# Seven half products for eight, moved from a kernel's second layer to the X and H parts of its first

## The chip, the cores and the metric

The kernel runs on one core of one Trainium2 chip, in one launch, in float32. The metric is the device time of the program in microseconds. The host only lays the inputs out.

## What is computed

The input x has 16 x 512 = 8192 rows of 512 values. Each row has a pathway token (500 kinds), a compartment token c (5) that also serves as its time step, and a mask bit that serves as its scale type m. The reference normalises the row, builds six blocks of 512 from it, weighs them by a softmax, puts them side by side (3072 values) and sends them through a network of two layers:

```python
h = _ln(x, pw_g[pathway_ids], pw_b[pathway_ids])
h = _ln(h, cp_g[compartment_ids], cp_b[compartment_ids])
t = _ln(x, tm_g[time_steps], tm_b[time_steps])
m = x + _mlp_ln(memory_state, ...)[:, None, :]       # n, r likewise from two other states
s = _ln(x, ms_g[scale_type], ms_b[scale_type])
cat = jnp.concatenate([w[0] * h, w[1] * t, w[2] * m, w[3] * n, w[4] * r, w[5] * s], axis=-1)
return x + _ln(silu(cat @ int_W1 + int_b1) @ int_W2 + int_b2, int_g, int_be)
```

## The kernel before, in words

**What is multiplied.** The six blocks come down to three parts of K = 512 each. Part X is x itself times one weight `wx_` (the blocks m, n and r share x). Part H is the twice normalised row times `wh_`. Part V is the once normalised row times a weight that depends on the row's two tokens (c, m): rows are sorted by these, so that a tile of 128 rows has (but for a few "extra" rows handled apart) one such weight, which is built for it as `vs = ws * s + wt * t` (`s_part` on ScalarE, `build` on VectorE). What is left of each block, with biases and the three states, is one row per kind, gathered from a table in DRAM (`gather_add`, the tile `add`).

**Tiles and windows.** The 8192 rows are 16 windows of four tiles of 128 rows. In each window four tiles are gathered (x by `gather_x`, the gains and shifts of the first norm by `gather_h`, which also gathers `cp`, those of the second), normalised, turned by VectorE's 32 x 32 transposes into `rX`, `rV`, `rH` (`turn`, L184), and spread by sixteen transfers for each part to `cX`, `cV`, `cH` (`spread_row`, L192, on SP's queue), so that K lies on the partitions. Layer 1 (`layer1`, L320) gives a tile 4 chunks x 3 parts of matmuls 128 x 128 times 128 x 512 into one PSUM tile. Then `hidden_add` (VectorE) adds the gathered row, `hidden_silu` (ScalarE) takes the activation, `turn_z` and `spread_row` make `cZ`, and layer 2 multiplies it by `w2`. `last_sum`, `last_var`, `last_pow` and `last_b` form the last norm, and `put_out` (GpSimd) scatters the rows to their places.

**Layer 2 before.** In windows 1 to 13 two tiles go together as a pair. Two tiles (rows), the two halves of K and the two halves of N make a 2 x 2 block product, done with seven half products for eight (Winograd's form): GpSimd forms sums of the operand in `z_sums` (L383 to L389, four of 128 x 256 for a pair), `weight_sums` formed those of `w2` once, `seventh` (L404, L406) multiplies with 256 columns, with the bias put in by a bfloat16 product of its own, and `keep_first`, `sum_first`, `keep_last` and `sum_last` (ScalarE copies, VectorE adds) put the four quarters together. In windows 0, 14 and 15 layer 2 is plain (`layer2`, L339).

**What sets the order.** Everything is issued in an order written out by hand as names: `ORDER` for the head, `WINDOW` once for each window (w = 0 to 14), `LAST` for the last. A name is a piece, a window (c the current, p the one before, n the next, o and m two before and after) and a tile or a pair and a number. Each engine and each DMA queue works its own pieces in this order; across engines they wait on semaphores. All normal transfers stand on SP's queue, all gathers and scatters on GpSimd's (POOL), among its arithmetic: `shift_x` (`sh`, L309), the powers (`fp`, `xp`, `lp`) and the sums.

Names that the prediction uses: `rd`, `la` reads of PSUM; `f1`, `f2` the two steps of the second norm on VectorE; `th`, `tv`, `tx`, `tz` transposes; `bd` build; `lb` end of the last norm; `gc`, `gh`, `ga`, `gx` gathers; `sh` shift_x; `sX`, `sZ` transfers; `p7`, `vp` products.

## Time and profile before

| | us |
|---|---|
| three runs | 976.53, 983.87, 984.45 |
| median | 983.87 |
| the profiled execution | 971.0 |
| its span, first to last instruction | 969.1 |
| TensorE busy in the span | 942.4 |
| VectorE busy | 820.2 |
| GpSimd busy | 653.1 |
| ScalarE busy | 571.5 |

The profile is of one execution. Busy time is the union of an engine's instruction records. A group's row gives line, engine, operation, out<-in, count, then busy time and mean ns of one, then the idle time of the engine ahead of it and what ended that. Records of instructions that follow each other overlap, as ends are pipelined; the pace is therefore read from the starts in the timeline. The mean granted clock of TensorE is 0.992.

### The profile page before, as it was taken

Reading aid. Unit: us, or ns where it says so; the run is one execution under the profiler, and the core shown is the slowest. Engines: PE = TensorE matmul, PEld = TensorE weight load, DVE = VectorE, ACT = ScalarE, POOL = GpSimd, SP = SyncE. Lnnn points to the kernel's source line nnn. Section 1 sums busy time; section 2 is a strip of 40 time slices with the busy share of each in tenths; the row PEclk is TensorE's granted clock in tenths of the full one; section 3 lists DMA queues with packets and bytes.
Section 4 is the critical chain, followed back from the end, with each engine's and each line's share of the span. In section 5 each row is a group of like instructions: output and inputs, shape, how many; then the busy total and the mean of one; then the engine's idle time right before and its main releaser. Section 6 shows DMA issues by size and latency. Waiting matters only on the chain.

```text
span 969.1 us, 11569 instructions
## 1 busy us (share of the span) xinstructions
PE 942.4 (97%) x2901; PEld 497.7 (51%) x2901; DVE 820.2 (85%) x1412; ACT 571.5 (59%) x1190; POOL 653.1 (67%) x697
## 2 busy tenths in 40 slices
...
GB/s 283 241 234 245 268 220 243 154 223 181 208 190 192 162 229 178 207 204 185 231 185 183 183 198 180 228 180 195 215 184 216 186 189 182 203 186 200 128 85 97
DMA packets 91885, 190.95 MB, mean 197 GB/s; under 512 B 25364, under 2 KB 25364, under 8 KB 91820
## 3 DMA queue, kind: packets, MB, share of 16 engines
...
## 4 chain that ended last, share of the span: by engine, by line
PE 84%; DVE 6%; DMA 5%; issue 2%; POOL 1%; SPq 1%; ACT 0%; POOLq 0%; ACTq 0%; DVEq 0%
PE p L320 62%; PE pq_0b L406 5%; PE pq_1b L406 5%; PE p L339 4%; PE pq_1a L406 3%; PE pq_0a L406 3%; DMA cH<-rH 2%; SPq L192 1%; DMA pw<-in_pw,i_pw 1%; DMA cX<-rX 1%; DVE vs L724 1%; POOL xbs L158 1%; DVE pw L283 0%; DMA pre<-diff_rows,tok_x 0%; DVE vs L226 0%
## 5 line engine op out<-in xcount | busy, mean ns | idle before, releaser
L320 PE MATMUL p<-wx__82,cX 128*128 128x512 f32 x512 | 227.9, 593 | 2.9 <-DVE adde L1118 2.9
L320 PE MATMUL p<-wh__83,cH 128*128 128x512 f32 x512 | 225.8, 593 | 1.8 <-DMA cH<-rH 1.7
L320 PE MATMUL p<-vs,cV 128*128 128x512 f32 x504 | 226.1, 592 | 0.0
L226 DVE SCALAR_TENSOR_TENSOR vs<-wt,sct,vs 128x512 f32<-128x512 f32 x252 | 175.8, 758 | 0.4 <-ACT vs L220 0.4
L220 ACT ACTIVATE vs<-ws,scs 128x512 f32<-128x512 f32 x252 | 164.1, 710 | 9.1 <-PE p L320 4.2
L320 PEld LDWEIGHTS p<-wx__82,cX 128*128 128x128 f32 x512 | 97.0, 190 | 125.3 <-issue 117.3
L320 PEld LDWEIGHTS p<-wh__83,cH 128*128 128x128 f32 x512 | 96.9, 190 | 114.6 <-issue 111.1
L320 PEld LDWEIGHTS p<-vs,cV 128*128 128x128 f32 x504 | 95.8, 190 | 115.0 <-issue 98.1
L327 ACT ACTIVATE add<-add 128x512 f32<-128x512 f32 x64 | 39.9, 625 | 158.2 <-DVE add L324 157.8
L497 POOL DMA_INDIRECT out<-yb,tok x64 | 71.5, 1116 | 76.4 <-DMA out<-yb,tok 27.9
L292 POOL TENSOR_TENSOR rsh<-veh,mhalf 128x1 f32<-128x1 f32 x64 | 42.3, 664 | 86.2 <-DVE vey L479 82.9
L158 POOL DMA_INDIRECT pw<-in_pw,i_pw x64 | 71.3, 1113 | 26.3 <-issue 12.5
L158 POOL DMA_INDIRECT xbs<-in_x,tok x64 | 68.4, 1069 | 24.3 <-issue 16.0
L309 POOL TENSOR_TENSOR xbs<-xbs,rows 128x512 f32<-128x512 f32 x64 | 81.7, 1279 | 0.8
L158 POOL DMA_INDIRECT add<-rows,i_add x64 | 69.0, 1078 | 16.6 <-issue 14.8
L158 POOL DMA_INDIRECT cp<-cp_rows,i_cp x64 | 63.3, 989 | 21.6 <-issue 17.7
L471 ACT ACTIVATE junk<-yb 128x512 f32<-128x512 f32 x64 | 39.9, 624 | 58.1 <-DVE yb L435 38.2
L324 DVE TENSOR_TENSOR add<-p,add 128x512 f32<-128x512 f32 x64 | 43.0, 673 | 24.7 <-PE p L320 24.6
L260 ACT ACTIVATE xm<-xbs,nmx,rsx 128x512 f32<-128x512 f32 x64 | 52.1, 815 | 19.7 <-DVE nmx L256 10.0
L296 ACT ACTIVATE pw<-pw,rsh 128x512 f32<-128x512 f32 x64 | 45.5, 713 | 26.4 <-POOL rsh L292 15.9
L301 DVE SCALAR_TENSOR_TENSOR pw<-pw,mvh,cp 128x512 f32<-128x512 f32 x64 | 60.4, 944 | 0.0
L238 ACT ACTIVATE junk<-xbs 128x512 f32<-128x512 f32 x72 | 44.7, 621 | 20.0 <-DMA xbs<-in_x,tok 19.0
...
## 6 DMA issues: line engine op xcount, KB each, us to landing
cV<-rV SPq DMA_DIRECT2D x256, 64.0 KB
cH<-rH SPq DMA_DIRECT2D x256, 64.0 KB
cZ<-rZ SPq DMA_DIRECT2D x256, 64.0 KB
...
```

What stands on the lines that cost most here:

```text
L158: nc.gpsimd.indirect_dma_start(dst, None, table, bass.IndirectOffsetOnAxis(ap=idx, axis=0), **kw)
L220: nc.scalar.activation(v[:, c], ws[:, c], AF.Identity, scale=scs[:, c, g, w : w + 1])
L226: nc.vector.scalar_tensor_tensor(v[:, c], wt[:, c], sct[:, c, g, w : w + 1], v[:, c], ALU.mult, ALU.add)
L238: nc.scalar.activation(junk, x, AF.Identity, accum_out=sums[:, 0, j : j + 1])
L260: nc.scalar.activation(t, st["xb"][:, j, :], AF.Identity, bias=st["nm"][:, j : j + 1], scale=st["rs"][:, j : j + 1])
L296: nc.scalar.mul(pw[:, :D], pw[:, :D], st.pop(("rs", j)))
L301: nc.vector.scalar_tensor_tensor(pw[:, :D], pw[:, :D], mv[:, 0, 0:1], cp, ALU.subtract, ALU.mult)
L309: nc.gpsimd.tensor_add(st["xb"][:, j, :], st["xb"][:, j, :], rows[:, 2, :])
L320: nc.tensor.matmul(st["p1", g], st["c" + blk][:, g, c, :], m[:, c, :], start=(blk == "X" and c == 0), stop=(blk == "H" and c == NC - 1))
L324: nc.vector.tensor_add(st["add", g], st["p1", g], st["add", g])
L406: nc.tensor.matmul(home, st["zp", p][k][:, c], at_["half"][k][:, c], start=False, stop=(c == 1), skip_group_check=True)
L497: nc.gpsimd.indirect_dma_start(out_rows, bass.IndirectOffsetOnAxis(ap=tok[:, j, w : w + 1], axis=0), yb[:, j, :], None)
```

## The change

- Layer 2 is plain again in all windows (`layer2`, then `last_add`); `z_sums`, `seventh`, the bias products and the four functions that put quarters together are gone.
- In windows 2 to 14 parts X and H of layer 1 together (K = 1024, of which X is the one half and H the other) become the 2 x 2 block product of a pair of tiles with seven half products (`xh_product`, 256 columns, four chunks each). The operand's sums are formed by GpSimd, in `cX` and `cH` themselves and in `s3` (four of 128 x 512 for a pair); those of `wx_` and `wh_` once in the head, in place, and undone ahead of the last window (`weights_back`).
- Part V is multiplied in two halves of N (`v_product`), one half into the banks of the pair's products, the other into a bank of its own.
- `hidden_add` is replaced in these windows by eleven adds of half width for a pair (`xh_read`), some of them between two products that add up in the same place.
- The mean and variance of the row ahead of the second norm come from two ScalarE passes (`front_sums`) for VectorE's batch statistics.
- The gather of `cp` is a step of its own (`gather_cp`), `cp` has two buffers for three; `xm` and `xn` share three buffers in place of two each; the two PSUM pools of four tiles become one of eight; `junk` is bfloat16; `ident` lives in the head only.
- `ORDER`, `WINDOW` and `LAST` are new.

```diff
 WINDOW = """
-    lX.c.3 lX.c.0 ha.p.3 hs.p.3 ga.c.2 lV.c.0 tz.p.2 xn.c.3 lb.o.3 gx.n.3 bd.c.1 xs.n.0 xn.c.2 po.o.2 sh.c.3 tz.p.3
-    xs.n.1 lX.c.1 lV.c.1 gx.n.2 gh.n.1 lX.c.2 f1.c.2 sp.c.2 sp.c.3 xs.n.3 f2.c.2 sZ.p.0 f1.c.3 f2.c.3 sZ.p.3 bd.c.2
-    lV.c.2 fp.c.3 fn.c.3 th.c.3 fp.c.2 po.o.3 ga.c.1 sZ.p.2 bd.c.3 xs.n.2 sZ.p.1 xe.n xp.n q7.p.1.1 zs.p.4 fn.c.2
-    th.c.2 sH.c.1 zs.p.0 zs.p.1 sp.n.0 sH.c.0 xm.n nv.n.1 tv.n.1 tx.n.2 q7.p.0.1 tx.n.1 zs.p.5 xn.n.1 q7.p.0.2
-    lV.c.3 kf.p.0 nv.n.3 kf.p.2 q7.p.0.5 tx.n.0 tx.n.3 kf.p.1 q7.p.1.5 zs.p.6 sH.c.3 sh.c.0 zs.p.7 f1.n.1 q7.p.1.6
-    nv.n.0 tv.n.3 sX.n.3 q7.p.0.7 ku.p.1 zs.p.2 q7.p.1.2 sf.p.2 kf.p.3 bd.n.0 q7.p.1.7 nv.n.2 tv.n.2 sH.c.2 f2.n.1
-    q7.p.0.6 q7.p.1.3 sX.n.1 sf.p.3 lH.c.1 ga.c.0 sh.c.1 tv.n.0 ha.c.1 lH.c.0 sl.p.2 ku.p.0 sf.p.1 sl.p.0 ha.c.0
-    zs.p.3 gh.n.0 q7.p.1.4 q7.p.0.4 gh.n.2 hs.c.1 xn.n.0 sl.p.3 lq.p.2 sf.p.0 lq.p.3 q7.p.0.3 sl.p.1 hs.c.0 sX.n.0
-    fp.n.1 lq.p.0 sh.c.2 fn.n.1 f1.n.0 lq.p.1 ga.c.3 lv.p tz.c.1 fp.n.0 lH.c.2 sp.n.1 th.n.1 ha.c.2 f2.n.0 lp.p
-    lb.p.1 sV.n.3 gh.n.3 hs.c.2 sV.n.1 po.p.1 lb.p.0 gx.m.0 sV.n.2 gx.m.1 sV.n.0 fn.n.0 lH.c.3 tz.c.0 lb.p.2 sX.n.2
-    po.p.0 th.n.0
+    gc.c.3 f1.c.3 p7.c.0.1 vp.c.0.0 xs.n.3 f1.c.2 sZ.p.1 gc.c.2 hb.c.3 xs.n.2 xe.n xp.n hb.c.2 po.o.3 xm.n vp.c.0.1
+    rd.c.0.0 sZ.p.0 p7.c.1.1 hv.c.3 vp.c.1.1 sZ.p.2 l2.p.1 ss.c.0.0 hv.c.2 sp.c.2 fp.c.3 la.p.1 nv.n.3 fp.c.2 xn.n.1
+    f2.c.2 sh.c.0 tv.n.3 nv.n.1 f2.c.3 sZ.p.3 tv.n.1 gc.n.1 gh.n.0 l2.p.0 la.p.0 ss.c.1.0 fn.c.3 th.c.3 l2.p.2
+    l2.p.3 fn.c.2 th.c.2 sH.c.3 f1.n.1 la.p.3 la.p.2 p7.c.0.7 nv.n.2 tv.n.2 rd.c.0.1 p7.c.1.7 sH.c.1 hb.n.1 hv.n.1
+    lq.p.3 vp.c.1.0 sh.c.2 lq.p.1 bd.c.2 rd.c.1.0 vp.c.2.1 lq.p.2 lq.p.0 rd.c.1.1 ss.c.1.1 sp.c.3 lv.p lp.p bd.c.3
+    tx.n.1 nv.n.0 gc.n.0 sH.c.2 p7.c.1.5 vp.c.3.0 ss.c.1.2 sH.c.0 xn.n.2 tv.n.0 f2.n.1 xn.n.0 lb.p.3 lb.p.0 tx.n.0
+    vp.c.3.1 sp.n.1 sV.n.3 rd.c.1.2 f1.n.0 rd.c.0.10 rd.c.0.9 hb.n.0 vp.c.2.0 fp.n.1 p7.c.0.2 lb.p.2 gh.n.3 ss.c.0.1
+    tx.n.2 sV.n.1 po.p.0 fn.n.1 gx.m.0 sV.n.0 sp.n.0 sV.n.2 lb.p.1 p7.c.1.2 tx.n.3 sX.n.0 ss.c.0.2 hv.n.0 ss.c.0.3
+    gx.m.1 ss.c.1.3 p7.c.0.5 rd.c.0.2 bd.n.0 gx.m.3 xn.n.3 rd.c.1.9 p7.c.1.6 rd.c.1.6 sX.n.2 p7.c.0.6 fp.n.0
+    rd.c.0.4 rd.c.1.3 p7.c.0.3 sh.c.1 sX.n.1 gx.m.2 xs.m.0 xs.m.1 gh.n.2 rd.c.0.5 rd.c.1.10 p7.c.1.3 po.p.1 rd.c.0.3
+    rd.c.1.7 ga.n.1 rd.c.1.5 th.n.1 rd.c.0.6 p7.c.0.4 rd.c.0.8 ga.n.2 hs.c.2 tz.c.2 sX.n.3 po.p.2 hs.c.1 p7.c.1.4
+    rd.c.0.7 rd.c.1.8 gh.m.1 ga.n.0 rd.c.1.4 ga.n.3 hs.c.3 f2.n.0 hs.c.0 tz.c.1 tz.c.3 tz.c.0 sh.n.3 fn.n.0 th.n.0
+    bd.n.1
 """
...
-    xnp = ctx.enter_context(tc.tile_pool(name="xnp", bufs=2))
+    xnp = ctx.enter_context(tc.tile_pool(name="xnp", bufs=3))
-    ps_1 = ctx.enter_context(tc.tile_pool(name="ps_1", bufs=4, space=bass.MemoryType.PSUM))
-    ps_2 = ctx.enter_context(tc.tile_pool(name="ps_2", bufs=4, space=bass.MemoryType.PSUM))
+    ps = ctx.enter_context(tc.tile_pool(name="ps", bufs=8, space=bass.MemoryType.PSUM))
...
+    def gather_cp(st, j):
+        w = st["w"]
+        st["cp", j] = cp = gp.tile([P, D], F32, tag="cp", name=f"cp{w}_{j}", bufs=2)
         gather(cp, cp_rows[:, :], i_cp[:, j, w : w + 1])
...
-        stats(mv, 0, pw[:, :D], P, "h")
+    def front_sums(st, j):
+        h = st["g", j][:, :D]
+        st["mv", j] = mv = small.tile([P, 3], F32, tag="mvh", name="mvh")
+        nc.scalar.activation(junk, h, AF.Identity, accum_out=mv[:, 0:1])
+        nc.scalar.mul(mv[:, 1:2], mv[:, 0:1], -1.0 / D)
+        nc.scalar.activation(junk, h, AF.Square, bias=mv[:, 1:2], accum_out=mv[:, 2:3])
...
+    def weight_sums(c):
+        H = D // 2
+        if "half" not in at_:
+            t = at_["late"].tile([P, 3, NC, H], F32, name="wxt")
+            at_["half"] = {1: wx_[:, :, :H], 2: wh_[:, :, :H], 3: wh_[:, :, H:], 4: t[:, 0], 5: wx_[:, :, H:],
+                           6: t[:, 1], 7: t[:, 2]}
+        b11, b21, b22, t4, t1, t2, t3 = [at_["half"][k][:, c] for k in range(1, 8)]
+        nc.gpsimd.tensor_sub(t3, b22, t1)
+        nc.gpsimd.tensor_sub(t1, t1, b11)
+        nc.gpsimd.tensor_sub(t2, b22, t1)
+        nc.gpsimd.tensor_sub(t4, b21, t2)
...
+    def xh_sums(eng, st, p, op):
+        t = xh_operands(st, p)
+        if op == 0:
+            eng.tensor_sub(t[-1], t[0], t[len(t) // 2])
+            return
+        a11, a12, a21, a22, _ = t
+        if op == 1:
+            eng.tensor_add(a21, a21, a22)
+        elif op == 2:
+            eng.tensor_sub(a11, a21, a11)
+        else:
+            eng.tensor_sub(a12, a12, a11)
...
+    def xh_product(st, p, k):
+        q1, q2 = xh_banks(st, p)
+        home = {1: q1[:, 0], 6: q1[:, 0], 2: q1[:, 1], 7: q2[:, 1], 4: q2[:, 1], 5: q2[:, 0], 3: q2[:, 0]}[k]
+        if k in (1, 5, 6):
+            m = st["cX"][:, 2 * p + (k == 5)]
+        elif k == 7:
+            m = st["s3"][:, p]
+        else:
+            m = st["cH"][:, 2 * p + (k == 4)]
+        for c in range(NC):
+            nc.tensor.matmul(home, m[:, c], at_["half"][k][:, c], start=(c == 0 and k in (1, 7)),
+                             stop=(c == NC - 1), skip_group_check=True)
+
+    def v_product(st, g, n):
+        p, b = divmod(g, 2)
         H = D // 2
+        q1, q2 = xh_banks(st, p)
+        home = v_bank(st, p)[:, b] if n else (q1, q2)[b][:, 1]
+        for c in range(NC):
+            nc.tensor.matmul(home, st["cV"][:, g, c], st["v", g][:, c, n * H : (n + 1) * H],
+                             start=(b == 0 and n == 1 and c == 0), stop=(c == NC - 1), skip_group_check=True)
+
+    def xh_read(st, p, i):
+        H = D // 2
+        q1, q2 = xh_banks(st, p)
+        a, b = st["add", 2 * p], st["add", 2 * p + 1]
+        half, bank = {0: (a[:, :H], q1[:, 0]), 1: (b[:, H:], q2[:, 1]), 2: (b[:, H:], q2[:, 0]),
+                      3: (a[:, H:], q1[:, 0]), 4: (b[:, :H], q1[:, 0]), 5: (b[:, H:], q1[:, 0]),
+                      6: (a[:, :H], q1[:, 1]), 7: (a[:, H:], q2[:, 0]), 8: (b[:, :H], q2[:, 1]),
+                      9: (a[:, H:], st.get(("pv", p), q1)[:, 0]), 10: (b[:, H:], st.get(("pv", p), q1)[:, 1])}[i]
+        nc.vector.tensor_add(half, bank, half)
```

Lines of the kernel after that the prediction names: L288 and L289 the two products of `front_1`, L312 `front_less`, L377 to L385 `xh_sums`, L427 `xh_read`.

280 lines of the change are left out of this document (110 added, 170 removed).

## The prediction

> **What bounds the kernel now.** I read the page's first part, then the busy time by stretches, then who waited for whom on TensorE, then TensorE's timeline.
>
> ```profile
> span 969.1 us, 11569 instructions
> PE 942.4 (97%) x2901; PEld 497.7 (51%) x2901; DVE 820.2 (85%) x1412; ACT 571.5 (59%) x1190; POOL 653.1 (67%) x697
> ```
> ```profile
> 0.00:100.00 100.00, 87.52 (x513) 53.52 (x514) 80.57 (x176) 79.26 (x194) 74.34 (x117) 0.95 0.82 252
> 100.00:200.00 100.00, 95.26 (x220) 41.13 (x220) 82.57 (x143) 52.58 (x97) 68.09 (x67) 1.00 0.77 218
> ```
> ```profile
> 207.00:877.00 670.00, 670.00 (x1956) 362.59 (x1955) 591.15 (x987) 402.19 (x825) 473.10 (x479) 1.00 0.69 195
> ```
> ```profile
> PE pc L660 <- DVE sm L666: 6.9, 1, 6.9
> ```
>
> In the rows of stretches the columns are start and end, length, then busy time of TensorE's matmuls, its weight loads, VectorE, ScalarE and GpSimd, the granted clock and the DMA share. From 207 to 877 us TensorE is busy for 670.00 of 670.00 us at a clock of 1.00. It is idle only in the head (12.5 us of the first 100, 4.7 of the second; the longest wait, 6.9 us, is its first) and behind the last product. So a window's time is TensorE's instruction count times their pace. VectorE comes next: 591.15/670 = 88%, which is 47.4 us of a window of 53.74. Pace and window come from the timeline:
>
> ```profile
> 575.15 3.60 PE L320 MATMUL p<-vs,cV 128*128 128x512 f32 x8
> 578.59 3.60 PE L320 MATMUL p<-wx__82,cX 128*128 128x512 f32 x8
> ...
> 592.32 0.28 PE L404 MATMUL pq_1a<-b2r,share 96*128 96x256 bf16 x1
> 592.43 1.03 PE L406 MATMUL pq_1a<-w,cZ 128*128 128x256 f32 x4
> ...
> 600.53 1.03 PE L406 MATMUL pq_1a<-w2t,zs 128*128 128x256 f32 x4
> 601.39 1.03 PE L406 MATMUL pq_0b<-w2t,zs 128*128 128x256 f32 x4
> ```
> ```profile
> 861.04 0.28 PE L404 MATMUL pq_1a<-b2r,share 96*128 96x256 bf16 x1
> ```
>
> An f32 matmul stands as two instructions. Eight with 512 columns step by 578.59 - 575.15 = 3.44 us, or 0.4294 each. Four with 256 columns step by 601.39 - 600.53 = 0.86, about 0.2155 each. Half the columns cost half, so products in half widths are nearly free of extra cost as long as the stream is unbroken. A bias product costs 592.43 - 592.32 = 0.11. The same product comes again five windows later, at 861.04: a window is (861.04 - 592.32)/5 = 53.74 us. The counts confirm the paces: 96 x 0.4294 + 56 x 0.2155 + 4 x 0.11 = 53.73.
>
> **TensorE's part of the change.** In a changed window (2 to 14, thirteen; layer 2 had its seven products in 1 to 13, thirteen too) layer 1 is 2 pairs x (7 products x 4 chunks + 16 for V) x 2 = 176 instructions of 256 columns: 37.93 us for 41.22. Layer 2 is 32 of 512 columns: 13.74 for 12.07 + 0.44. Sum 51.67 against 53.73: 2.06 a window, 26.8 in all. This is the gain if nothing makes TensorE wait.
>
> **What the others get.**
>
> ```profile
> L226 DVE SCALAR_TENSOR_TENSOR vs<-wt,sct,vs 128x512 f32<-128x512 f32 x252 | 175.8, 758 | 0.4 <-ACT vs L220 0.4
> L301 DVE SCALAR_TENSOR_TENSOR pw<-pw,mvh,cp 128x512 f32<-128x512 f32 x64 | 60.4, 944 | 0.0
> L283 DVE TENSOR_TENSOR pw<-xn,pw 128x512 f32<-128x512 f32 x64 | 51.3, 801 | 5.3 <-ACT xn L260 2.7 <-DMA pw<-in_pw,i_pw 2.5
> L284 DVE TENSOR_TENSOR pw<-pw 128x512 f32<-128x512 f32 x64 | 49.6, 775 | 2.2
> L163 DVE BATCH_NORM_STATS2 sth<-pw 128x6 f32<-128x512 f32 x64 | 44.5, 695 | 2.2
> L164 DVE BATCH_NORM_AGGREGATE mvh<-sth 128x2 f32<-128x6 f32 x64 | 11.7, 182 | 2.2
> L324 DVE TENSOR_TENSOR add<-p,add 128x512 f32<-128x512 f32 x64 | 43.0, 673 | 24.7 <-PE p L320 24.6
> L433 DVE TENSOR_TENSOR yb<-yb 128x256 f32<-128x256 f32 x26 | 21.8, 838 | 1.4
> L435 DVE TENSOR_TENSOR yb<-yb,pq_0b 128x512 f32<-128x512 f32 x13 | 8.9, 688 | 9.2 <-PE pq_0b L406 9.2
> L309 POOL TENSOR_TENSOR xbs<-xbs,rows 128x512 f32<-128x512 f32 x64 | 81.7, 1279 | 0.8
> L383 POOL TENSOR_TENSOR zs<-cZ 128x256 f32<-128x256 f32 x26 | 18.3, 718 | 0.3
> L389 POOL TENSOR_TENSOR zs<-cZ,zs 128x256 f32<-128x256 f32 x26 | 25.7, 990 | 0.0
> L238 ACT ACTIVATE junk<-xbs 128x512 f32<-128x512 f32 x72 | 44.7, 621 | 20.0 <-DMA xbs<-in_x,tok 19.0
> ```
> ```profile
> 607.46 0.70 DVE L301 SCALAR_TENSOR_TENSOR pw<-pw,mvh,cp 128x512 f32<-128x512 f32 x1
> 608.09 0.41 DVE L424 TENSOR_TENSOR yb<-yb,pq_1b 128x256 f32<-128x256 f32 x1
> 608.42 0.70 DVE L184 STREAM_TRANSPOSE rV<-xm 128x512 f32<-128x512 f32 x1
> 609.34 0.69 DVE L324 TENSOR_TENSOR add<-p,add 128x512 f32<-128x512 f32 x1 [0.22 <-PE p L320]
> 609.95 0.41 DVE L433 TENSOR_TENSOR yb<-yb 128x256 f32<-128x256 f32 x1
> 610.28 0.42 DVE L424 TENSOR_TENSOR yb<-yb,pq_0b 128x256 f32<-128x256 f32 x1
> 610.80 1.60 DVE L433 TENSOR_TENSOR yb<-yb 128x256 f32<-128x256 f32 x1
> ```
> ```profile
> 608.05 0.95 POOL L158 DMA_INDIRECT pw<-in_pw,i_pw  x1 [0.30 <-issue]
> 609.31 0.96 POOL L158 DMA_INDIRECT cp<-cp_rows,i_cp  x1 [0.30 <-issue]
> 610.84 1.27 POOL L309 TENSOR_TENSOR xbs<-xbs,rows 128x512 f32<-128x512 f32 x1
> ```
>
> VectorE's starts lie closer than its durations: a half-width add leads the next by 0.33 us (608.09 to 608.42), a full add or a transpose by 0.61 (609.34 to 609.95), a scalar-tensor-tensor by 0.63 (607.46 to 608.09). In a window it loses 4 statistics with their aggregates (0.695 + 0.182), 4 hidden adds (0.61), 4 half adds that end layer 2 (0.33), 2 sums of L433 (0.838) and 2 of L435 (0.61): 3.5 + 2.4 + 1.3 + 1.7 + 1.2 = 10.1. It gets 22 half-width reads of PSUM (`rd`) and 4 full adds (`la`): 7.3 + 2.4 = 9.7. That makes 47.0 of 51.67, where it had 47.4 of 53.74: its free time goes from 6.3 to 4.7.
>
> ScalarE gets the statistics, two passes of 0.62 or a little more for each tile (L238 is such a pass), and loses six half copies: it has 402.19/670 = 60% now, 32 us of a window, and stays under 40, covered. GpSimd's eight sums grow from 256 columns to 512: about 0.85 each (between L383 and L389) become 1.28 (L309), 3.4 more on 37.9 (473.10/670 of 53.74), so 41 of 51.67. The transfers are as many as before on the same queues. The gather of `cp` becomes a step of its own: POOL's queue is put in another order, not lengthened. SP's queue takes no new transfer, but its last sixteen of a window (`sX`) now wait for the last product that reads `cX`, `p7.c.0.6`, which ends 44.8 us into the window by the paces above.
>
> ```profile
> 602.00 2.42 SPq L192 DMA_DIRECT2D cX<-rX  x4
> ```
>
> Sixteen take 9.7, until 2.9 us into the next window; the four `sZ` behind them until 5.3, and layer 2 needs them at 8.6: covered, with 3.3 left for their landing. The weights' sums are sixteen of 256 columns in the head (11.5 us at 0.72) for four of 512 and the bias parts, on a GpSimd that is 68% busy there (second row of the stretches), and `wr` at the end stands beside layer 2: no cost.
>
> The buffers (three for `xn` and `xm` together, two for `cp`, one pool of eight in PSUM) cost nothing by themselves, only through the circles below.
>
> **The price: VectorE held up by GpSimd.** In the row at 610.80 an add that took 0.41 us at 609.95 takes 1.60, and ends just after GpSimd's sum (610.84 + 1.27 = 612.11). Adds that read PSUM do not show it: L324's mean, 0.673, is no longer than its single row at 609.34. What this costs now:
>
> ```profile
> L301 DVE SCALAR_TENSOR_TENSOR pw<-pw,mvh,cp x64: 702/741/2452, 64.7 to 906.8; 128x512 f32<-128x512 f32 x64
> ```
> In a window L301 loses 4 x (0.944 - 0.741) = 0.8 us so. L433 loses 2 x (0.838 - 0.41) = 0.85; L283 and L284, of the shape of L435 with its 0.688, lose 4 x (0.113 + 0.087) = 0.8; L226 at most 16 x (0.70 - 0.68) = 0.3. That is 2.7 a window, while GpSimd's sums run 4 x 1.28 + 8 x 0.85 = 11.9 us. With the change they run 12 x 1.28 = 15.4. In proportion that gives 3.5, a little less because L433 is gone: I take 3.2. The bounds are 1.8 (L433's part goes, nothing grows) and 7.7 (each of twelve catches an operation for half its length, 0.64). I stay near the lower one, as the operations that can be caught are those of these rows. The 47.0 above holds 1.8 already, so VectorE needs 48.4.
>
> The Trainium skill (SBUF — State Buffer, Who interferes with whom) has it as a lock: "A DVE instruction with two SBUF inputs contends with a GpSimd instruction that reads SBUF", and the loser waits out the whole instruction; the trace agrees (1.60 against 0.41 us). By that rule the 22 new PSUM reads are safe and the eight longer sums are not, which speaks against the change: taken to its end it is rival (c).
>
> **Two circles.** Each engine works its queue in order, so what counts is the longest circle through a window. (1) Layer 2's last product -> `la.p.3` on VectorE -> all of its queue to the last chunk of `bd.n.1` -> `vp` of tile 1 in the next window -> four layer-2 products. On VectorE: 2 la (1.2), 21 rd (6.9), 12 transposes (7.3), 2 f2 (1.3), one f1 (1.4), 4 lb (5.5), 16 chunks of build at 0.68 (10.9; 175.8/252 = 0.70 with L226's own hold-ups), small ones 0.5: 35.0. Then 0.43 for the last chunk, 13.74 for layer 2, 0.4 for hand-overs (the 0.22 of row 609.34, twice): 49.6, plus its share of the hold-ups, 2.6: 52.2. (2) `th.n.0` on VectorE frees a `pw` buffer -> POOL's queue: `gh`, two `ga`, `sh`, `gc`, `gc` -> landing -> `f2.c.2` -> VectorE to `th.n.0`.
>
> ```profile
> cp<-cp_rows,i_cp POOLq DMA_INDIRECT x64, 5.5
> add<-rows,i_add POOLq DMA_INDIRECT x64, 4.3
> ```
>
> Gathers leave 1.26 apart (608.05 to 609.31): 4 x 1.25 + 1.28 + a landing between 4.3 and 5.5 (`cp` stands behind the twice larger `pw` today, as `add` does not; I take 4.9) = 11.2; VectorE from `f2.c.2` to `la.p.3` 5.7 (2 f2, 4 transposes, a la, an f1), then the 35.0 without `bd.n.1`'s 2.7, together 38.0; hand-overs 0.3: 49.5, plus 3.0 of hold-ups: 52.5. Both pass TensorE's 51.67, so TensorE will wait about 0.8 a window. 53.74 - 52.5 = 1.24, x 13 = 16 us.
>
> **Sum.** Head and tail keep their matmuls; their orders are new, and TensorE's 17 us of head idle can move either way: taken as zero, 6 us each way in the range. The profiled execution took 971.0 us (span 969.1 and 1.9 around it); the runs' median, 983.87, is 1.3% above. The gain is taken off the median: 968. With hold-ups of 2.3 to 3.7 in the second circle this case spans 959 to 977.
>
> **Rivals.** (a) TensorE never waits: the planned order has enough room, as it had before (88% on VectorE, no wait in 670 us). For it: VectorE still has 51.67 - 48.4 = 3.3 us free. Against: the circles have only about 2 us of room for hold-ups. 983.9 - 26.8 = 957. (b) The circle through the gather is the long one with the 5.5 landing and hold-ups of 3.5: 53.6, gain 2 us: 982. For it: DMA is 0.69 busy. (c) Slower: GpSimd's sums catch VectorE two times in three at half length, 12 x 2/3 x 0.64 = 5.1: 54.6 a window, 0.9 x 13 = 11 us: 995. It decides from hold-ups of 4.2 a window on. For it: L301 already loses 2.452 - 0.741 = 1.7 us in its worst case. Against: now there are twelve such sums too, and they cost 2.7. (d) A doubled pace of 256 columns by weight loads is excluded: 0.2155 is measured.
>
> **Chances.** Forecast 0.36, (a) 0.26, (b) 0.19, (c) 0.19. The range from 953 to 990 leaves out the end of (a) and most of (c). A measurement of this kernel tells about 1% from no change: below 974 lie (a) and three quarters of the forecast, 0.53; within 1% 0.28; above 994 0.19, with the head's losses.
>
> **What would show it.** Steps of TensorE's timeline of 0.2155 and 0.4294 unchanged; window starts 52.5 apart; new TensorE waits on `vs` (build) and `cZ` of about 0.8 a window; L288, L312 (products ahead of H) longer than their medians beside POOL's sums at L377 to L385, PSUM reads at L427 not. Wrong would be: no waits at all (then 957), waits on POOL's sums themselves, or a head longer by over 6 us.

## The result and the profile after

| | before | after |
|---|---|---|
| median of 4 runs, us | 980.2 (976.08 to 984.45) | 1132.06 (1131.24 to 1134.16) |
| ratio, 95% interval | | 1.155 (1.148 to 1.162) |
| profiled span | 969.1 | 1129.5 |
| window (2 to 14) | 53.74 | 63.47 |
| span outside thirteen windows | 270.5 | 304.3 |

The change costs 152 us; 968 was predicted. The predicted window was 52.5 us. A window of the kernel after is read from one start of layer 2 in TensorE's timeline (222.76 us) to that thirteen windows later (1047.92). The page's first part, then the busy time of that stretch and of what lies outside it (columns as in the prediction):

```profile
span 1129.5 us, 13393 instructions
PE 986.7 (87%) x3577; PEld 652.2 (58%) x3577; DVE 920.4 (81%) x1466; ACT 656.2 (58%) x1432; POOL 712.8 (63%) x702
```
```profile
222.76:1047.92 825.16, 727.30 (x2682) 522.83 (x2681) 718.10 (x1106) 482.54 (x1036) 541.41 (x489) 0.96 0.59 164
```
```profile
0.00:222.76 222.76, 193.06 (x753) 101.03 (x754) 165.03 (x306) 153.89 (x355) 147.13 (x190) 0.94 0.74 221
1047.92:1129.50 81.58, 66.35 (x144) 28.32 (x144) 37.31 (x54) 19.75 (x44) 24.22 (x24) 0.90 0.26 78
```

825.16/13 = 63.47 us, 10.97 over the predicted 52.5. TensorE, never idle before, is idle for 825.16 - 727.30 = 97.9 us, and its matmuls take 727.30 for 13 x 51.67 = 671.7 at full pace, 55.6 us more. By the granted clock (0.96 on average) about 0.04 x 825 = 33 us of these are time lost at a lower clock, an estimate; the rest is not taken apart here. VectorE is busy for 718.10/13 = 55.2 us a window, where it was 47.4. The miss is (63.47 - 52.5) x 13 = 143 in the windows, 304.3 - 270.5 = 34 outside them, less the 13 by which the prediction's base, the median, stood above the profiled execution.

Who waits for whom, TensorE first, then VectorE in the thirteen windows (us in total, times, longest):

```profile
PE pq_0b L416 <- DVE add L427: 22.7, 13, 1.9
PE pq_1b L407 <- DVE add L427: 20.4, 12, 2.8
PE pq_0b L407 <- DVE add L427: 16.1, 8, 2.3
PE pq_1b L407 <- POOL s L377: 14.8, 12, 3.4
```
```profile
DVE nmx L261 <- POOL rsx L253: 43.8, 12, 6.1
DVE pw L312 <- DMA cp<-cp_rows,i_cp: 21.5, 13, 2.3
DVE vea L249 <- ACT junk L245: 19.4, 8, 2.4
DVE add L427 <- PE pq_1b L407: 1.4, 3, 0.7
```

TensorE waits mostly for VectorE's reads of PSUM (59.2 us in these rows), and 14.8 us for the first of GpSimd's sums (L377); VectorE waits for TensorE 1.4 us in 825. So TensorE no longer sets the pace. VectorE does, with 55 us of work a window and 63.47 - 55.2 = 8.2 us of standing still, in which it waits for GpSimd's power, the gather of `cp` and ScalarE's row sums. TensorE's waits, and with them its lower clock, follow from this. The groups of VectorE's work:

```profile
L231 DVE SCALAR_TENSOR_TENSOR vs<-wt,sct,vs 128x512 f32<-128x512 f32 x252 | 225.1, 952 | 0.0
L289 DVE TENSOR_TENSOR pw<-pw 128x512 f32<-128x512 f32 x64 | 77.6, 1213 | 2.2
L427 DVE TENSOR_TENSOR add<-pq_1a,add 128x256 f32<-128x256 f32 x65 | 26.7, 411 | 0.4
```

Build's mean went from 758 to 952 ns; the second step of the first norm, L289, from 775 (L284 before) to 1213. The reads of PSUM (L427) stay at 0.41. The trace's records, counted one by one, show that this is no general slowing: of the 208 builds in the thirteen windows, the 45 that overlap one of GpSimd's sums take 1.83 us on average, the other 163 take 0.74. The time by which such an instruction is longer is called a hold-up below. One such place, VectorE's rows first, then GpSimd's:

```profile
554.89 3.09 DVE L289 TENSOR_TENSOR pw<-pw 128x512 f32<-128x512 f32 x1
```
```profile
554.93 1.27 POOL L377 TENSOR_TENSOR s<-cX 128x512 f32<-128x512 f32 x1
556.15 1.27 POOL L320 TENSOR_TENSOR xbs<-xbs,rows 128x512 f32<-128x512 f32 x1
```

An add that takes 0.69 undisturbed (row at 601.86 below) takes 3.09 here and ends (557.98) after the second of two sums that follow each other (557.42). In the kernel before, fewer sums lie beside such instructions: of 192 builds in twelve windows, 8 overlap a sum. A part of its sums runs where VectorE turns tiles, with one input each, and nothing is held up there; GpSimd's rows of one such place of before, then VectorE's:

```profile
594.17 1.41 POOL L383 TENSOR_TENSOR zs<-cZ 128x256 f32<-128x256 f32 x2
595.66 1.42 POOL L385 TENSOR_TENSOR cZ<-cZ 128x256 f32<-128x256 f32 x2
```
```profile
595.79 0.71 DVE L184 STREAM_TRANSPOSE rV<-xm 128x512 f32<-128x512 f32 x1 [0.88 <-ACT xm L260]
596.42 2.45 DVE L184 STREAM_TRANSPOSE rX<-xbs 128x512 f32<-128x512 f32 x4
```

Counted over these windows, GpSimd's sums run beside VectorE instructions with two inputs in SBUF for 5.0 of their 11.9 us a window before, and for 11.9 of 15.7 after.

The boundary between two windows in the kernel after, VectorE (the transpose at 596.60 is `th.n.0`, the row at 601.86 the end of `f1.c.2`, that at 612.01 the first `f2`), then GpSimd:

```profile
596.60 0.67 DVE L186 STREAM_TRANSPOSE rH<-pw 128x512 f32<-128x512 f32 x1
...
601.86 0.69 DVE L289 TENSOR_TENSOR pw<-pw 128x512 f32<-128x512 f32 x1
604.98 0.98 DVE L249 TENSOR_SCALAR vea<-sums 128x4 f32<-128x4 f32 x1 [2.43 <-ACT junk L245]
609.43 0.16 DVE L261 TENSOR_TENSOR nmx<-sums,rsx 128x4 f32<-128x4 f32 x1 [3.47 <-POOL rsx L253]
...
612.01 0.75 DVE L312 SCALAR_TENSOR_TENSOR pw<-pw,mvh,cp 128x512 f32<-128x512 f32 x1 [1.36 <-DMA cp<-cp_rows,i_cp]
```
```profile
599.24 1.54 POOL L489 DMA_INDIRECT out<-yb,tok  x1 [1.82 <-DMA out<-yb,tok]
601.08 0.98 POOL L160 DMA_INDIRECT pw<-in_pw,i_pw  x1 [0.30 <-issue]
...
606.09 0.97 POOL L160 DMA_INDIRECT cp<-cp_rows,i_cp  x1 [0.16 <-issue]
...
608.34 1.06 POOL L253 TENSOR_TENSOR rsx<-vea,mhalf 128x4 f32<-128x4 f32 x1
```

VectorE stands still here for 2.43 + 3.47 + 1.36 = 7.3 us, of 8.2 in a mean window: the power that it needs is queued behind a scatter, a `gh`, two `ga`, a shift and two `gc`.

### The profile page after: what moved, and what is told of

It is laid out like the page before. It is cut to its first block, busy times and chain, and to the rows that moved or that the text cites. A ratio compares the mean times of both kernels' runs of the same rounds, so it can differ in the third digit from the quotient of the medians.

```text
span 1129.5 us, 13393 instructions
## 1 busy us (share of the span) xinstructions
PE 986.7 (87%) x3577; PEld 652.2 (58%) x3577; DVE 920.4 (81%) x1466; ACT 656.2 (58%) x1432; POOL 712.8 (63%) x702
## 5 line engine op out<-in xcount | busy, mean ns | idle before, releaser
L351 PE MATMUL p<-w,cZ 128*128 128x512 f32 x512 | 225.9, 595 | 10.1 <-DMA cZ<-rZ 7.1
L231 DVE SCALAR_TENSOR_TENSOR vs<-wt,sct,vs 128x512 f32<-128x512 f32 x252 | 225.1, 952 | 0.0
L351 PEld LDWEIGHTS p<-w,cZ 128*128 128x128 f32 x512 | 95.4, 190 | 133.6 <-issue 132.0
L294 ACT ACTIVATE junk<-pw 128x512 bf16<-128x512 f32 x64 | 40.2, 629 | 162.8 <-issue 100.9
L416 PE MATMUL pqv<-vs,cV 128*128 128x256 f32 x416 | 107.5, 398 | 0.4 <-DVE vs L231 0.4
L160 POOL DMA_INDIRECT xbs<-in_x,tok x64 | 71.2, 1113 | 51.3 <-DVE yb L485 30.8
L312 DVE SCALAR_TENSOR_TENSOR pw<-pw,mvh,cp 128x512 f32<-128x512 f32 x64 | 71.2, 1113 | 27.0 <-DMA cp<-cp_rows,i_cp 26.4
L416 PEld LDWEIGHTS pqv<-vs,cV 128*128 128x128 f32 x416 | 81.4, 200 | 19.6 <-DVE vs L231 7.9
L289 DVE TENSOR_TENSOR pw<-pw 128x512 f32<-128x512 f32 x64 | 77.6, 1213 | 2.2
L308 ACT ACTIVATE pw<-pw,rsh 128x512 f32<-128x512 f32 x64 | 44.0, 711 | 51.5 <-DVE pw L312 45.1
L484 DVE SCALAR_TENSOR_TENSOR yb<-yb,rsy,rows 128x512 f32<-128x512 f32 x56 | 70.0, 1250 | 1.0 <-POOL rsy L476 1.0
L243 ACT ACTIVATE junk<-xbs 128x512 bf16<-128x512 f32 x72 | 44.8, 623 | 33.3 <-DMA xbs<-in_x,tok 31.9
L407 PE MATMUL pq_0b<-wh__80,cH 128*128 128x256 f32 x104 | 35.4, 500 | 27.8 <-DVE add L427 16.1
L381 POOL TENSOR_TENSOR cX<-cX,cH 128x512 f32<-128x512 f32 x26 | 35.2, 1354 | 36.3 <-DMA cH<-rH 33.6
L463 ACT ACTIVATE junk<-yb 128x512 bf16<-128x512 f32 x64 | 40.3, 630 | 28.2 <-DVE yb L458 26.4
```

Of the source, the lines that this page charges most:

```text
L160: nc.gpsimd.indirect_dma_start(dst, None, table, bass.IndirectOffsetOnAxis(ap=idx, axis=0), **kw)
L231: nc.vector.scalar_tensor_tensor(v[:, c], wt[:, c], sct[:, c, g, w : w + 1], v[:, c], ALU.mult, ALU.add)
L243: nc.scalar.activation(junk, x, AF.Identity, accum_out=sums[:, 0, j : j + 1])
L289: nc.vector.tensor_add(pw[:, :D], pw[:, :D], pw[:, D:])
L308: nc.scalar.mul(pw[:, :D], pw[:, :D], st.pop(("rs", j)))
L312: nc.vector.scalar_tensor_tensor(pw[:, :D], pw[:, :D], st["mv", j][:, 1:2], cp, ALU.add, ALU.mult)
```

## The experiments

Theory H: GpSimd's sums hold VectorE up, and that is the loss. Rival O: the new order is too long by itself. Rival K: the lower clock of TensorE after its waits makes the loss. After four runs H and O each had part of it, and O was split into V (VectorE's standing still at the boundary, the circle through GpSimd's gathers) and S (SP's queue). "Before" on the same chips took 974 to 983 us. A window is the stretch between layer 2's starts divided by 13 (in e4, between starts of its first product, by 12); VectorE's busy time is that stretch's, divided likewise. "Fills" are memsets, which write a constant and read nothing, so kernels with fills leave the operand's sums out. Each of e1 to e18 was executed once, e14 and e17 four times.

| run | us | window | VectorE busy |
|---|---|---|---|
| after | 1132.06 | 63.47 | 55.2 |
| e1: eight sums as fills | 1039.86 | 56.78 | 45.1 |
| e2: all sums as fills | 1037.75 | 57.25 | 44.4 |
| e3: sums on VectorE | 1087.87 | 60.41 | 52.8 |
| e4: before, with more sums | 997.39 | 55.13 | 48.8 |
| e5: after, sZ from ScalarE | 1173.75 | 66.23 | 54.5 |
| e6: e2, sZ from ScalarE | 1098.62 | 60.66 | 44.6 |
| e7: first new boundary | 1104.70 | 62.02 | 54.1 |
| e8: e7, sums on VectorE, sZ from ScalarE | 1125.05 | 62.67 | 51.7 |
| e9: second new boundary | 1067.98 | 59.59 | 52.6 |
| e10: e9 with fills | 1029.86 | 56.88 | 44.5 |
| e11: e2, one product moved | 1004.64 | 54.99 | 44.3 |
| e12: e9, sums on VectorE | 1050.33 | 58.21 | 51.8 |
| e13: e10 and e11 | 1008.04 | 54.82 | 44.5 |
| e14: e12, one product moved | 1044.53 | 57.30 | 51.8 |
| e15: e9, one product moved | 1078.92 | 59.99 | 52.9 |
| e16: e13, two more moved | 1001.36 | 54.66 | 44.7 |
| e17: e14, two more moved | 1093.73 | 61.54 | 52.7 |
| e18: e13, a layer-2 tile later | 1050.64 | 58.14 | 44.9 |

### The sums as fills (e1, e2)

```diff
-        if op == 0:
-            eng.tensor_sub(t[-1], t[0], t[len(t) // 2])
...
+        m = t[-1] if op == 0 else t[(2, 0, 1)[op - 1]]
+        eng.memset(m, 0.01)
+        eng.memset(m, 0.01)
```
e2 also has, in `shift_x`:
```diff
-        nc.gpsimd.tensor_add(st["xb"][:, j, :], st["xb"][:, j, :], rows[:, 2, :])
+        nc.gpsimd.memset(st["xb"][:, j, :], 0.5)
+        nc.gpsimd.memset(st["xb"][:, j, :], 0.5)
```

> The eight sums of a window at L377 to L385 are replaced by two fills each of the same target (a fill of 128x512 took 0.57 us in the head, so two take 1.14 for a sum's 1.28): GpSimd is occupied about as long, at the same place of its queue, but reads nothing. The operand's sums are thereby left out. Theory H (a sum of GpSimd's that reads SBUF holds VectorE's two-operand instructions up for nearly its whole length; 10.9 us a window now, by twelve sums): four sums a window are left, so hold-ups fall to about 10.9 x 4/12 = 3.6 us and the window from 63.5 to 53 to 55 us; 13 x 9 = 117 us less, 1005 to 1030 us. Theory O (the new order's circles, by landings, buffers and GpSimd's queue, are too long by themselves): GpSimd's queue is as long as before, so windows stay at 60 us or more and the time over 1085. Theory K (the granted clock after waits makes the loss): clock and waits go together, so it agrees with H on the time, but under it windows with waits left still show halved pace.

> As the run before, and shift_x (L320) is a pair of fills as well, so no long GpSimd instruction reads SBUF at all; the operand's sums and the shift are left out. Theory H: hold-ups under 1 us a window, window 51.7 to 52.5 (TensorE's own 51.67 and a little), time 985 to 1000 with the head and tail as they are (some 34 us longer than before). Theory O: windows of 60 us or more, over 1085 us.

Measured: 1039.86 and 1037.75 us. The stretch of thirteen windows of e2, and two of its groups of VectorE:

```profile
217.79:962.02 744.23, 695.04 (x2680) 512.04 (x2681) 577.02 (x1107) 484.78 (x1040) 490.89 (x645) 0.98 0.65 182
```
```profile
L231 DVE SCALAR_TENSOR_TENSOR vs<-wt,sct,vs 128x512 f32<-128x512 f32 x252 | 174.7, 755 | 0.0
L289 DVE TENSOR_TENSOR pw<-pw 128x512 f32<-128x512 f32 x64 | 45.6, 712 | 2.2
```

VectorE's busy time goes from 718.10 to 577.02 us with the same instructions: 141.1/13 = 10.9 us a window were hold-ups, and without them it needs 44.4. A pair of fills is nearly as long in GpSimd's queue as a sum (0.54 + 0.53 for 1.28). It writes and doesn't read, and VectorE isn't held up: the 41 builds beside a fill take 0.74 us, like those beside nothing. The Trainium skill (SBUF — State Buffer, Who interferes with whom) says that a two-input VectorE instruction contends with a GpSimd instruction that reads SBUF and not with one that only writes it, and the trace agrees (755 for 952 ns). The fills change two things beside this: GpSimd is busy for 541.41 - 490.89 = 50.5 us less, and they don't wait for the landing of `cH`, as L381 does in the kernel after (33.6 us). That isn't what the window gained, as VectorE's stops are as long as with the sums: 43.7 us for the power, 19.2 for `cp` and 38.0 for the row sums, where they were 43.8, 21.5 and 37.4. H is thus shown for 63.47 - 57.25 = 6.2 us of a window. But both runs stay above what H expected (1005 to 1030, 985 to 1000): e2 at 57.25 a window, not 52, though VectorE stands still for 57.25 - 44.4 = 12.9 us of it. e1 tells the same: four shifts still read, yet the hold-ups are 45.1 - 44.4 = 0.7 us and the window is no longer than e2's. Something else limits at 57.

### The sums on VectorE, and more sums in the old order (e3, e4)

```diff
-    "ss": lambda st, p, k: xh_sums(nc.gpsimd, st, p, k)
+    "ss": lambda st, p, k: xh_sums(nc.vector, st, p, k)
```
e4 is the kernel before, with a second copy of the instruction in `z_sums` for three of its four sums:
```diff
             nc.gpsimd.tensor_sub(s2, a21, a11)
+            nc.gpsimd.tensor_sub(s2, a21, a11)
```

> The eight sums of a window go to VectorE (each some 0.61 us there), at the same places of the order. VectorE's need becomes 47 + 8 x 0.61 = 51.9 us a window plus the hold-ups that the four shifts still make. Theory H: 3.6 us of hold-ups for 10.9, so 55.5 to 57.5 a window and 1035 to 1060 us, faster than with the sums on GpSimd although VectorE has more to do. Theory O: VectorE is fuller by 4.9 us, so windows of 64 us or more and over 1130 us.

> The kernel before, with three of four of its layer-2 sums issued twice with the same operands and target (6 more a window, of 0.72 to 0.99 us: GpSimd's sums take some 17 us a window for 11.9, more than the 15.4 of the kernel after). The result is unchanged. If the catch is a property of the old order (23% of the sums' length, 2.7 of 11.9), hold-ups come to 3.5 to 4.5 us a window and the time stays within 1% of before, as VectorE has 6.3 us free. If any added sum is caught for nearly its whole length (theory H without regard to the order), hold-ups come to 7.5 to 8 us a window, past the free 6.3, and TensorE waits 1 to 3 us a window: 990 to 1020 us.

e3: 1087.87 us, 44 less than after, though VectorE has eight more instructions a window. Its hold-ups are what H expected, 52.8 - 44.4 - 8 x 0.61 = 3.5 us for 3.6; the window is longer than expected (60.4 for 55.5 to 57.5), as VectorE still stands still for 60.4 - 52.8 = 7.6 us. e4: 997.39 us. Twelve windows of it, then twelve of before:

```profile
224.23:885.79 661.56, 650.22 (x1873) 345.97 (x1872) 585.38 (x953) 386.89 (x794) 513.76 (x529) 1.00 0.68 191
```
```profile
216.11:861.04 644.93, 644.93 (x1874) 347.50 (x1872) 569.41 (x950) 386.52 (x793) 451.78 (x456) 1.00 0.69 196
```

GpSimd works (513.76 - 451.78)/12 = 5.2 us a window more, VectorE (585.38 - 569.41)/12 = 1.3 more: a quarter of the added sums is caught, about what the prediction took as the proportion (2.7 of 11.9). In the old order that proportion holds. In the new one 10.9 of 15.7 is caught, 69%. The time rose by 1.4% (a window of 55.13 us for 53.74), beyond the expected 1% and into the range of the other case (990 to 1020), but not by that case's hold-ups of 7.5 to 8 us: the product waits for its operand, which is queued longer on GpSimd.

```profile
PE pq_0a L409 <- POOL zs L389: 7.9, 12, 1.0
```

### A test that said nothing of the other limit: sZ from ScalarE's queue (e5, e6)

```diff
-            nc.sync.dma_start(st[cat][q * L : (q + 1) * L, g]...
+            (nc.scalar if cat == "cZ" else nc.sync).dma_start(st[cat][q * L : (q + 1) * L, g]...
```

> The kernel after, with the sixteen sZ transfers of a window issued from ScalarE's queue for SP's; nothing else. Theory V (in the kernel after, VectorE's queue is the circle: 55 us of work with hold-ups and 8 us of standing still while it waits in turn for ScalarE's statistics, GpSimd's power and the landing of cp; TensorE's waits and its halved clock only follow): no change, windows 62.5 to 64.5, 1115 to 1145 us. Theory S (SP's queue, 48 transfers in a row from the last product that reads cV, is what makes the window long): sixteen transfers fewer on SP, at 0.63 each, shorten the window by 3 us or more, under 1095 us.

> The kernel whose sums and shift are fills (1037.75 us, 57.2 us a window; the operand's sums and the shift are left out), with the sixteen sZ transfers issued from ScalarE's queue. There TensorE waits for cZ and the chain runs through SP's queue: sV, sX and four of sZ, 36 x 0.635 = 22.9 us, behind the last product that reads cV. Theory S: with 32 for 36 and no queue behind sX, the circle falls below the gather's one (15.4 + 38.0 = 53.4 us); windows 52 to 54.5, clock 0.98 or more, 975 to 1005 us. If the landing of cZ itself, or tz on VectorE, were what is late: windows stay at 56 to 58, 1025 to 1045.

Both missed: 1173.75 (42 us more) and 1098.62 (61 more). ScalarE's own work came to stand behind the transfers that it issues. A wait of it in e6, ahead of its part of the build:

```profile
ACT vs L225 <- DMA cZ<-rZ: 56.7, 13, 4.6
```

The statistics (L294) wait 45.1 us more in the same way: about 8 us a window together. VectorE in turn stands still for 60.66 - 44.58 = 16.1 us a window, 3.2 more than in e2. The edit brought a cost of its own, so it says nothing on S either way.

### VectorE's standing still (e7, e8, e9, e12)

e7 and e9 move names at the boundary of windows (and, to match, at the start of `LAST`); e9's edit:

```diff
-    gc.c.3 f1.c.3 p7.c.0.1 vp.c.0.0 xs.n.3 f1.c.2 sZ.p.1 gc.c.2 hb.c.3 xs.n.2 xe.n xp.n hb.c.2 po.o.3 xm.n vp.c.0.1
-    rd.c.0.0 ...
+    f1.c.3 p7.c.0.1 vp.c.0.0 xs.n.3 f1.c.2 sZ.p.1 xs.n.2 hb.c.3 xe.n xp.n po.o.2 gh.n.1 sh.c.3 hb.c.2 po.o.3 vp.c.0.1
+    rd.c.0.0 xm.n ...
...
-    ... sX.n.3 po.p.2 hs.c.1 p7.c.1.4
-    rd.c.0.7 rd.c.1.8 gh.m.1 ga.n.0 rd.c.1.4 ga.n.3 hs.c.3 f2.n.0 hs.c.0 tz.c.1 tz.c.3 tz.c.0 sh.n.3 fn.n.0 th.n.0
+    ... sX.n.3 hs.c.1 p7.c.1.4
+    rd.c.0.7 rd.c.1.8 ga.n.0 rd.c.1.4 hs.c.3 f2.n.0 gc.n.3 gc.n.2 ga.n.3 hs.c.0 tz.c.1 tz.c.3 tz.c.0 fn.n.0 th.n.0
```
e7 has `gc.n.3 gc.n.2 po.p.2 gh.m.1 ga.n.0 ga.n.3` at the second place instead, and so no `po.o.2 gh.n.1` at the first.

> The kernel after in a changed order at the window's boundary only: the two gathers of cp stand ahead of po, gh and two ga on GpSimd's queue for behind them, the power of the first norm ahead of shift_x for behind it and the two gathers, and ScalarE's last row sums of x ahead of the first statistics of H. Same instructions, all sums on GpSimd. Theory V: VectorE's standing still at the boundary falls from 8.2 us a window to between 1.5 and 3.5, the window to 57 to 59.5 (hold-ups stay), the time to 1045 to 1080. If hold-ups alone were the limit (theory H), or TensorE's halved clock (theory K): hold-ups of 10.9 stay, and the time stays over 1110.

> All three together, with the right result: the new order at the boundary, the eight sums on VectorE and sZ from ScalarE's queue. VectorE needs 47.0 + 8 x 0.61 = 51.9 us, hold-ups by the four shifts 0.6 to 3, standing still 1.5 to 3: windows of 54 to 57.5, 1005 to 1060 us. Under 1000 would mean that VectorE's need is smaller than summed; over 1070 that a further circle exists.

e7 missed: 1104.70 us, 62.0 a window. The three old stops are gone and one took their place: `add`, whose gathers e7 had put last.

```profile
DVE add L427 <- DMA add<-rows,i_add: 79.3, 11, 8.1
```

e8 missed too (1125.05): it has that fault and the one of e5. e9 puts `add` and `cp` first:

> The kernel after with the boundary's order changed once more: both gathers of add and of cp ahead of po.2 and gh on GpSimd's queue (in the order before this one, add stood behind them and VectorE waited 6.6 us a window for its landing), the power ahead of po, gh and shift_x, ScalarE's row sums of x ahead of those of H. All sums stay on GpSimd. Theory V: standing still under 3 us a window, hold-ups as before at 10 to 11, windows 57 to 59.5, 1050 to 1080 us. If a further circle of about 61 us stands behind it (last transpose of Z, sZ, layer 2, la, VectorE's queue): 60 to 61.5 a window, 1085 to 1110.

> The new boundary order with the eight sums on VectorE, right result: VectorE's need 51.9 us a window, hold-ups of the four shifts 0.6 to 3, standing still under 3: 54.5 to 58 a window, 1010 to 1060 us; with a further circle of about 61: over 1085.

e9: 1067.98 us, e12: 1050.33. e9's stretch and what VectorE still waits for:

```profile
217.14:991.75 774.61, 704.80 (x2680) 519.73 (x2681) 684.17 (x1107) 483.97 (x1037) 541.61 (x490) 0.97 0.61 175
```
```profile
DVE yb L458 <- PE p L351: 32.0, 24, 2.0
DVE rH L186 <- ACT pw L308: 19.2, 10, 2.8
DVE veh L300 <- ACT junk L296: 12.5, 13, 1.7
DVE nmx L261 <- POOL rsx L253: 12.0, 13, 1.7
```

The power's stop falls from 43.8 to 12.0 us, that for `cp` from 21.5 to 1.1, and the window loses 63.47 - 59.59 = 3.9 us with all sums on GpSimd. But VectorE's standing still falls only from 8.2 to 59.59 - 52.63 = 7.0 us a window: it now waits for layer 2, which is behind `cZ` (L458), and for ScalarE (L308, L296). The other 2.6 of the 3.9 are hold-ups, 684.17/13 - 44.4 = 8.2 for 10.9, as the order also changed what stands beside the sums (8.9 us beside two-input instructions for 11.9). So V is shown in part: the order opens the stops at the boundary, and the next circle takes most of their place. e9's time lies in V's range by luck, with more standing still than the 3 us expected and fewer hold-ups than the 10 to 11; e12's time lies in its range too, at 58.2 a window and with 6.4 us of standing still. K isn't borne out as the cause in the kernel after: of VectorE's 8.2 us of standing still a window there, 0.1 ends with TensorE.

### SP's queue (e10, e11, e13, e14, e15)

In e2, SP's queue, then TensorE's timeline at both ends of it:

```profile
530.91 10.67 SPq L194 DMA_DIRECT2D cV<-rV  x16
541.74 10.13 SPq L194 DMA_DIRECT2D cX<-rX  x16
551.98 10.34 SPq L194 DMA_DIRECT2D cZ<-rZ  x16
```
```profile
528.99 1.89 PE L410 MATMUL pq_1a<-vs,cV 128*128 128x256 f32 x8
...
558.17 14.30 PE L352 MATMUL p<-w,cZ 128*128 128x512 f32 x32 [2.39 <-DMA cZ<-rZ]
```

The last product that reads `cV` frees it at 530.7. Then sixteen `sV`, sixteen `sX` and the first four `sZ` go out one behind the other, until about 554.6, and layer 2 starts 3.6 us later, at 558.17: 27.5 us in all. Layer 2 (13.74) and eight products (13.8) lead back to the freeing of `cV`. That makes 55.0; the mean window of 57.25 is 2.2 longer, which this sum leaves open. TensorE waits for `cZ` 33.5 us in the thirteen windows, in 16 places. e11 moves one product out of this circle:

```diff
-    ... sH.c.2 p7.c.1.5 vp.c.3.0 ...
-    vp.c.3.1 sp.n.1 sV.n.3 rd.c.1.2 f1.n.0 rd.c.0.10 rd.c.0.9 hb.n.0 vp.c.2.0 fp.n.1 p7.c.0.2 ...
+    ... sH.c.2 vp.c.3.0 ...
+    vp.c.3.1 sp.n.1 sV.n.3 f1.n.0 rd.c.0.10 rd.c.0.9 hb.n.0 vp.c.2.0 p7.c.1.5 fp.n.1 p7.c.0.2 rd.c.1.2 ...
```

> The same new order with all GpSimd sums as fills (operand's sums and shift left out), so without hold-ups and with a short boundary. Theory S (SP's queue from the last product that reads cV through sV, sX, sZ and layer 2 is what is left at 57.2 us): nothing of that is touched, 55 to 57.5 a window, 1010 to 1040 us. If the boundary was what is left: 52 to 54, under 1000.

> All GpSimd sums as fills in the old boundary order (1037.75 us, 57.2 us a window), with one product, p7.c.1.5, moved from ahead of the last product that reads cV to behind it, so that sV can start 1.73 us earlier. Theory S: the window falls by 1.7 us, and by up to 2 more where the wait for cZ goes and the granted clock stays up behind it: 990 to 1017 us. If SP's queue isn't the circle: 1033 to 1042.

e10: 1029.86 us, 56.88 a window: with no hold-ups the boundary is worth 0.4 us. e11: 1004.64, 54.99: moving one product of 1.73 us gains 2.26 a window, and VectorE's wait for layer 2 falls from 50.3 us to 7.1 in the thirteen windows. S is shown for the kernels without hold-ups.

> All three removed: sums and shift as fills (the operand's sums and the shift are left out), the second new boundary order, and p7.c.1.5 behind the last product that reads cV. If these three are all: VectorE has 5 us of room, the gather's circle is under 50, and SP's is 1.7 shorter than 55.3: windows of 51.7 to 54, clock over 0.985, 970 to 992 us. If a further circle is left: 54.5 or more, as without the boundary order (1004.64), over 998.

> Right result: sums on VectorE, the second boundary order, p7.c.1.5 moved. VectorE needs 51.9 us and 2.6 of hold-ups by the shifts; TensorE waited 1.8 us a window for cZ and 2.2 for VectorE before this step. If SP's queue was the longer circle there: 55 to 57 a window, 1010 to 1037 us. If VectorE's queue was: 58, 1045 to 1055.

> Right result, all sums on GpSimd: the second boundary order and p7.c.1.5 moved. VectorE's need of 47 with hold-ups of 8 to 10 makes 55 to 57; it stood still for 7 us a window in the same order, of which la behind cZ made 2.5. Windows of 56.5 to 59, 1030 to 1062 us; SP's share here is smaller than without the sums, as VectorE's queue is nearly as long. No change (1064 to 1072) would mean that VectorE's queue alone limits it.

e13 came out in its other case, with a further circle: 1008.04, 54.82 a window. With real sums the same steps make e14, the fastest of the versions that compute everything: 1044.53 us, ratio to before 1.065 (1.059 to 1.071), so still slower than before. It lies between its two expected cases, next to the one in which VectorE's queue is the limit. e15 lies above both of its ranges: 1078.92, 11 more than e9, of which 7 can be the chip's (before took 982.86 there and 976.01 beside e9). With the hold-ups in place the moved product gains nothing.

### What holds the window at 54.7 (e16, e17, e18)

> As the run with all three removed (1008.04 us, 54.8 a window; operand's sums and shift left out), with p7.c.0.2 and p7.c.1.2, which read cH, moved behind p7.c.0.6, the last product that reads cX, so that sX can start 3.46 us earlier. Theory S: the window falls by 2.5 to 3.1, to 51.7 to 52.3 us, TensorE's own, clock over 0.985: 965 to 978 us. If a further circle is left: no less than 54, over 995.

> The same move in the kernel with real sums on VectorE (1044.53 us, 57.3 a window; right result). If la behind the late cZ (3.3 us a window of VectorE's standing still) goes: 54 to 55.5 a window, 1003 to 1022 us. If the sums on VectorE come too late for the products that are now earlier, or VectorE's queue is the limit: 56.5 or more, 1034 to 1055.

```diff
-    ... vp.c.2.0 p7.c.1.5 fp.n.1 p7.c.0.2 rd.c.1.2 ... lb.p.1 p7.c.1.2 tx.n.3 ... p7.c.1.6 rd.c.1.6 sX.n.2 p7.c.0.6 fp.n.0
-    rd.c.0.4 rd.c.1.3 ...
+    ... vp.c.2.0 p7.c.1.5 fp.n.1 rd.c.1.2 ... lb.p.1 tx.n.3 ... p7.c.1.6 sX.n.2 p7.c.0.6 fp.n.0
+    p7.c.0.2 p7.c.1.2 rd.c.0.4 rd.c.1.6 rd.c.1.3 ...
```

e16 came out in its other case too: 1001.36, 54.66. Its SP queue:

```profile
622.82 10.29 SPq L194 DMA_DIRECT2D cV<-rV  x16
633.27 10.04 SPq L194 DMA_DIRECT2D cX<-rX  x16
```

`sX` starts when the last `sV` has gone out, 622.82 + 10.29 = 633.11, and not when `cX` is free: two gates stood at the same place, and the edit opened the one that didn't decide. e17 is no test: behind its move, product 2 reads `cH` after the third sum has been written into it, so it multiplies another operand, and TensorE waits for the sums on VectorE, 54.3 us in thirteen places. Its 1093.73 us lie above both expected ranges.

> The run with all three removed (1008.04 us, 54.8 a window; operand's sums and shift left out), with one of the four layer-2 tiles (l2.p.3, 3.43 us of TensorE) and what follows it (la.p.3, the last norm) moved behind the last product that reads cV, so that sV, and with it sX, sZ and the next layer 2, can start 3.4 us earlier. Theory S with cV as its gate: windows of 51.7 to 53, 965 to 985 us, TensorE's waits for cZ nearly gone. If the window stays at 54 or more (over 995), a circle is left that isn't SP's queue.

```diff
-    ... l2.p.2 l2.p.3 ... la.p.3 la.p.2 ... lq.p.3 ... lv.p lp.p ... lb.p.3 lb.p.0 ... vp.c.2.0 p7.c.1.5 ...
+    ... l2.p.2 ... la.p.2 ... vp.c.2.0 l2.p.3 la.p.3 lq.p.3 p7.c.1.5 ... lv.p lp.p rd.c.1.2 lb.p.3 lb.p.0 ...
```

1050.64, worse: the last norm's power now waits on GpSimd's queue for its input, with all gathers behind it.

```profile
POOL rsy L470 <- DVE vey L465: 144.1, 13, 12.4
```

So it isn't settled whether SP's queue is the last circle at 54.7, or another of nearly that length stands beside it.

## Why the prediction was wrong

- **TensorE's part: right.** Layer 2 runs 32 instructions in 13.74 us (539.52 to 553.26 in its timeline) and a product eight in 1.73; 51.67 a window is its work at full pace.
- **VectorE's need: right.** 47.0 with 1.8 of hold-ups in it, so 45.2; without hold-ups 44.4 is measured (e2).
- **The hold-ups: this step failed.** "In proportion that gives 3.5, a little less because L433 is gone: I take 3.2." Measured: 10.9 us a window (after against e2), beyond the upper bound of 7.7 too. The mechanism was the right one, and rival (c), with a chance of 0.19, named it with its place and sign; it priced it at 5.1. Two things were wrong. The proportion of 23% belongs to the old order (e4: still a quarter with 5.2 us more of sums), not to the kernel: there the sums run beside two-input instructions for 5.0 of 11.9 us, and the new order puts them beside builds, `f1` and the last norm, for 11.9 of 15.7. And "half its length" was no upper bound: an instruction can wait for two sums in a row (3.09 for 0.69 us).
- **Circle (2): too short on both legs.** From the end of `th.n.0` (597.27) to `f2` (612.01) it took 14.7 us for 11.2: a scatter, `po.p.2`, stands in GpSimd's queue ahead of `gh` and waits for the scatter before it (1.82 us), so that `gh` (601.08) follows this scatter and not the freeing of its buffer by `th.n.0`; and `f2` starts 5.9 us behind the issue of `cp`, where the forecast had 4.9 for its landing. The rest of the window, VectorE's leg, is 63.5 - 14.7 = 48.8 for 41.3, 7.5 more, as the hold-ups are 10.9 for the 3.0 that were put there. e2 takes the hold-ups away and gains 6.2; e9 moves the queue of the first leg and gains 3.9, 2.6 of it hold-ups. They don't add up (57.25 to 56.88 for the boundary when the hold-ups are gone), because S stands near 57.
- **SP's queue: "covered, with 3.3 left for their landing" failed too, without effect on the time.** Layer 2 starts 3.6 us behind the issue of the fourth `sZ` (e2), a little more than the 3.3; and what was left out is that `sX` stands behind sixteen `sV`, which wait for the last product that reads `cV`. As VectorE's circle is longer, it shows only once that is shortened.
- **TensorE waits of 0.8 a window on `vs` and `cZ`: wrong.** They are 97.9/13 = 7.5, most of it for VectorE's reads (59.2 us for L427, and 11.7 that the profile puts down to L300, which VectorE works between such reads). 6.9 us are for `cZ` and 1.6 for `vs`. Another 14.8 are waits for GpSimd's sum L377, which the prediction had named as a sign of being wrong. The lower clock behind the waits was not in the prediction; it is no cause here, since VectorE hardly waits for TensorE.
- **Head and tail "taken as zero": 34 us.** Outside the thirteen windows there are 304.3 us for 270.5. The first layer 2 starts 14.6 us later, so much of it arises in the head; a head longer by over 6 us was the other named sign of being wrong. Before, then after:

```profile
174.91 13.90 PE L339 MATMUL p<-w,cZ 128*128 128x512 f32 x32
```
```profile
189.46 13.97 PE L351 MATMUL p<-w,cZ 128*128 128x512 f32 x32 [0.18 <-DMA cZ<-rZ]
```

  Of e9's 1066.2 us 774.61 lie in its thirteen windows, leaving 291.6; in e2 291.8 are left. So 13 of the 34 go with either edit; the other 21 stay in both, and their cause is open.
- **What would show it:** L312 is longer (mean 1113 ns for 944) and the PSUM reads are not, as said; L288 hardly (746), and most of the loss is in L231 and L289, and in the last norm (L484, 1250 ns for 735 beside fills).
